# A third sequence's gathers beside the first experts, and an earlier order of fetches in the second attention

## The chip, the cores and the metric

The kernel runs on one core of one Trainium2 chip. The measure is device time in microseconds (us) of one execution; lower is better. Several executions of each kernel are timed, and one more is recorded by the hardware profiler. The engines are called as in the profile: PE is TensorE (matrix multiply; PEld are its weight loads), DVE is VectorE, ACT is ScalarE, POOL is GpSimd, SP is SyncE, which here only issues DMAs. Each engine works through its own instructions in order, and they wait for each other on semaphores. DMAs are issued by SP (plain copies) and by POOL (indirect ones, with an address for each row), and run on 16 DMA engines.

## What is computed

Eight sequences of 512 tokens with 256 features pass through two layers. Each layer is an attention and then a mixture of experts, both with a layernorm ahead and a residual:

```python
x = x + _L0_attn_ref(_layernorm(x, axis=-1), ...)   # 16 heads, 4 key/value heads, rotary, causal
x = x + _L0_ffn_ref(_layernorm(x, axis=-1), ...)    # 32 experts of width 96, 8 per token, weighted sum
x = x + _L1_attn_ref(_layernorm(x, axis=-1), ...)   # 16 heads, causal, biases
x = x + _L1_ffn_ref(_layernorm(x, axis=-1), ...)    # 16 experts of width 176, 2 per token, and a shared one
```

Attention mixes tokens within one sequence only. The experts treat every token by itself: a router picks 8 of 32 (in the second layer 2 of 16) experts for a token, and its result is the weighted sum of theirs.

## The kernel before

**Four stages.** First attention with the first router; first experts; second attention with the second router and the shared expert; second experts. In the profiled execution they take roughly 0 to 370, 370 to 820, 820 to 1366 and 1366 to 1597 us. The attentions go sequence by sequence. The experts go over tiles of 128 rows: the attention stage has scattered each token's row, once for every expert chosen, into a slab of that expert in memory (`xg`, L456 on POOL), and a table says which expert each tile belongs to.

**The first experts (`experts`, L1205).** Two tiles are one job. A job runs through five stages, each a fixed number of steps behind the one before: load the rows from `xg` (SP, L1244), transpose them (PE, L1258), gate and up products (L1290), transpose (L1309), down product (L1319). The result is copied out of PSUM by ACT (`ys`, L1324) and stored to `yg` in memory (SP, L1327). There are 139 jobs, so 146 steps. The order of PE's instructions is fixed by hand; the other engines' order is made by the framework from the order of the code and the dependencies.

**The gathers (`gathers`, L1394).** A token's eight expert results lie in eight rows of `yg`. They are added to its `x` by indirect DMAs with an add: one for each of the 8 choices and each of the 4 groups of 128 tokens, 32 for a sequence, all issued by POOL at L1399. Each fetches 128 rows of 1 KB. Four gathers later the next one adds to the same rows of `x`, and waits until the earlier one has landed. Before that, SP has to fetch `x` itself as it stood after the first attention (`fetch_x`, L168, from `x_after`).

**What may run beside the experts (`Beside`, L1180).** Side work is given as a generator with a first step, a last step and a number of pieces; `Beside.step` takes as many pieces at each expert step as keep it even. `x_in_ring` (L1565) is such work: it fetches `x` of the first `AHEAD` sequences and then makes their gathers, two for each piece, and each of these waits for the last `ys` copy of its step. It runs from step `n_early // 2 + 8` = 83 to the end, 145. Sequences below `AHEAD` read only the first `n_early` = 150 tiles of `yg` (`most_rows`, L1359), which are stored by then; a sequence that isn't read so early waits for all of `yg`. The weights of the second attention are loaded beside these steps too (from step 69).

**The second attention (`planned`, L816).** An outer loop runs over the sequences b = 0 to 7. Each iteration has 12 stages, one for each entry of `PLAN1`; in each, PE makes one block of scores for the heads, and then letters say what side work goes with it: `p` is a piece of the preparation of sequence b + 1 (its layernorm, which reads the gathered `x`, and its projections), `a` and `o` are pieces of the output, the router and the shared expert of sequences b - 1 and b - 2, `g` is a piece of the chain `ahead`, and `m`, `c`, `t` belong to the scores. At the start of each iteration, `ahead` is made for sequence b + `AHEAD` = b + 2: `ahead1` (L1671) fetches its `x`, loads one part of the second experts' gate and up weights (SP), and makes its 32 gathers. The parts are `NB - AHEAD` = 6.

**Five places for x.** `new_x` (L161) takes its tiles from a ring of five. The second attention's sequences 0 to 4 find their places free; sequence 5 has to wait until sequence 0 is through the router and the shared expert and has been copied to memory (`keep_x`, L1687), sequence 6 for sequence 1, and sequence 7 for sequence 2.

**Scatters of the second router.** The router makes 8 scatters for a sequence (2 choices, 4 groups) and appends them to the list `waiting`; in each of the 12 stages `send` issues up to `SENT[1][n]` = 2 of them on POOL, without further waits in this layer.

The lines that steer this:

```python
SENT = ((3, 3, 2), (2, 2, 2))
AHEAD = 2
beside.add(done, end_done, AHEAD * 16 + 1, x_in_ring())        # L1611
"a": chain(finish, b - 1), "g": chain(ahead, b + AHEAD),       # L830
load_gate_up(gw1, f1, I1, N1R, b - AHEAD, NB - AHEAD)          # L1675
```

Marks that are used below: L787 is the first VectorE instruction of a sequence's output, once for each sequence; L344 on `stats_a` is the first step of the layernorm ahead of the second attention; L507 adds the shared expert's result; L735 masks the scores.

Of the kernel before, what the change touches and what calls it, by code (L numbers as in the profile page):

```python
# [8 lines left out]
F32 = mybir.dt.float32  # L9
# [8 lines left out]
P = 128  # L18
NB, T, D = 8, 512, 256
NT = T // P  # L20
# [13 lines left out]
PLAN1 = "cooggm oggm toggm coaggm aopggm taaoggm cppaoggm ppoggm taaopggm caopm aopam tapopm"  # L34
TAIL1 = "otaaoaaaoaoaoaa"
PB = (3, 2)
SENT = ((3, 3, 2), (2, 2, 2))
SPLIT = (4, 6)
AHEAD = 2
GU0, GU1 = ND * 2 * I0, ND * 2 * I1  # L40
ND1 = 2
NS = -(-IS1 // P)
# [56 lines left out]
def two_blocks_kernel(  # L99
# [18 lines left out]
    xpool = ctx.enter_context(tc.tile_pool(name="x", bufs=1, reuse_waits="tile"))  # L118
# [39 lines left out]
    xs = {}  # L158
    x_after = [drp.tile([NB, P, NT * D], F32, tag=f"x_after{n}", name=f"x_after{n}") for n in range(2)]

    def new_x(b, name):  # L161
        xs[b] = xpool.tile([P, NT, D], F32, tag="x", name=f"x_{name}_{b}", bufs=5)
        return xs[b]

    def keep_x(b, dram):
# [2 lines left out]
    def fetch_x(b, dram, name):  # L168
        return nc.sync.dma_start(out=new_x(b, name).rearrange("p t d -> p (t d)"), in_=dram[b]).ins
# [641 lines left out]
    def send(n, pace):  # L811
        for work, t, i in waiting[:n]:
            work(t, i, pace)
        del waiting[:n]

    def planned(att, before, after, plan, tail, ahead=None):  # L816

        def finish(b):
            yield from att.output(b, xs[b])
            yield from after(b)  # L820

        def chain(make, b):
            return make(b) if make and 0 <= b < NB else iter(())

        drain(before(0))
        old, next_one = iter(()), chain(before, 1)
        for b in range(NB):
            chains = {
                "p": next_one, "q": chain(before, b + 2), "o": old,
                "a": chain(finish, b - 1), "g": chain(ahead, b + AHEAD),  # L830
            }
            for at, works in enumerate(plan.split()):
                c, n = divmod(at, len(BANKS))
                if n == 0:
                    att.head(b, c)
                att.scores(b, c, n, att.probs)
                send(SENT[att.n][n], None if att.n else att.newest)
                for work in works:
                    if work == "c":
                        att.products()  # L840
                    elif work == "t":
                        att.turn()
                    elif work == "m":
                        att.mask(n, att.probs)
                    else:
                        next(chains[work], None)
            for work in "pog":
                drain(chains[work])
            next_one, old = chains["q"], chains["a"]
        att.held = att.made  # L850
        att.products()
        chains = {"o": old, "a": finish(NB - 1)}
        for work in tail:
            if work == "t":
                att.turn()
            else:
                next(chains[work], None)
        for work in "oa":
            drain(chains[work])
        if att.n:  # L860
            send(len(waiting), None)
# [497 lines left out]
    def most_rows(b, again):  # L1359
        lay = lays[0]  # L1360
        return (lay.most_tiles if again else lay.n_early if b < AHEAD else lay.n_tiles) * P

# [31 lines left out]
    def gathers(b, again="", pace=None):  # L1394
        lay = lays[0]
        rows = lay.rows[b]
        for i in range(lay.k):
            for t in range(NT):
                inst = nc.gpsimd.indirect_dma_start(  # L1399
                    out=xs[b][:, t, :], out_offset=None, in_=lay.yg[: most_rows(b, again), :],  # L1400
                    in_offset=bass.IndirectOffsetOnAxis(ap=rows[:, t, i : i + 1], axis=0), compute_op=ALU.add,
                )
                if pace:
                    tc.add_manual_dep(inst.ins, pace().name, SYNC, reason="gathers come evenly beside the tiles")
                if t % 2:
                    yield
# [43 lines left out]
    def load_x(b, tmp, bank, xf=None):  # L1450

        new_x(b, "in")
        xf = xf or read_x(b, tmp)
        for h in range(NT // 2):
            tr = bank(f"xin_{b}_{h}").rearrange("p (t d) -> p t d", t=2)
            for i in range(2):
                for c in range(ND):
                    t = 2 * h + i
                    nc.tensor.transpose(tr[:, i, c * P : (c + 1) * P], xf[:, c, t * P : (t + 1) * P], ident)
            nc.scalar.copy(xs[b][:, 2 * h : 2 * h + 2, :], tr)  # L1460
            yield
# [51 lines left out]
    def drain(part):  # L1513
        for _ in part:
            pass
# [31 lines left out]
    def all_experts(n, gw, gat, again=False, weights=()):  # L1547
# [6 lines left out]
        with ExitStack() as s:  # L1554
# [10 lines left out]
            def x_in_ring():  # L1565
                for b in range(AHEAD):
                    fetch_x(b, x_after[0], f"a1{g}")
                yield
                for b in range(AHEAD):
                    yield from gathers(b, g, None if again else lambda: beside.made)  # L1570

            def all_places():
                for b in range(NB):
                    yield from places(b, gat, g, beside.last)
# [34 lines left out]
            if n == 0:  # L1609
                beside.add(*((end + 1, end + 2) if again else (known, done - 2)), NB, all_places())  # L1610
                beside.add(done, end_done, AHEAD * 16 + 1, x_in_ring())  # L1611
            else:
# [17 lines left out]
    with ExitStack() as s2:  # L1630
        lasting.append(s2.enter_context(tc.tile_pool(name="xn_rows", bufs=2, reuse_waits="tile")))
        PARTS = 4
        with ExitStack() as s:
            awp, lnp, atp, late, ptp, smp, ps = pools(s, 0, False)
            bank = banks(ps, 3)
            att, before = fast0(awp, lnp, atp, late, ptp, ps, bank)
            route, _ = ffn_parts(smp, bank)
            gw0 = gpool.tile([P, E0 * GU0], F32, tag="gu", name="gw0")

            def after0(b):  # L1640
                if b == NB - 1:
                    return
                kept = keep_x(b, x_after[0])
                yield from routed0(b, lnp, bank, route)
                if b < PARTS:
                    with tc.issue_after(kept):
                        load_gate_up(gw0, f0, I0, N0, b, PARTS)
                if b == 1:
                    yield from biases1(smp, bank)
                if b == SPLIT[0] - 1:  # L1650
                    yield from tables(lays[0], smp, bank, 0)


            with tc.manual_schedule(engines={ENG.PE}):
                planned(att, before, after0, PLAN0, TAIL0)


        with ExitStack() as s1:
# [4 lines left out]
            with ExitStack() as s:  # L1663
# [7 lines left out]
                def ahead1(b):  # L1671
                    if b >= AHEAD:
                        fetched = fetch_x(b, x_after[0], "a1")
                        with tc.issue_after(fetched):
                            load_gate_up(gw1, f1, I1, N1R, b - AHEAD, NB - AHEAD)  # L1675
                        yield
                        yield from gathers(b)
# [13 lines left out]
                with tc.manual_schedule(engines={ENG.PE}):  # L1691
                    planned(att, before, after1, PLAN1, TAIL1, ahead1)
# [246 lines left out]
```

## Time and profile before

| | |
|---|---|
| median of 3 runs | 1592.55 us (1592.25 to 1599.87) |
| the profiled execution | 1599.16 us, of which the span on the core is 1597.4 |
| mean granted clock of PE | 0.956 |
| PE busy | 1429.2 us, 89% of the span |
| DVE, ACT, POOL busy | 954.7, 667.1, 805.5 us |
| gathers (L1399), on POOL | 256, together 403.5 us |
| scatters (L456), on POOL | 320, together 322.4 us |
| DMA | 240.36 MB, mean 150 GB/s |

The table of groups gives, for a line, the busy time, the mean of one in ns, and the idle time of its engine just before, with what ended it. The table by stretch gives for each stretch the busy time of each engine and the number of its instructions, then the granted clock of PE (1.00 is full), the share of time in which the 16 DMA engines were busy with packets (it can pass 1, as packets overlap), and what they moved. In a timeline each row is a start, a duration, the instruction, and in brackets how long the engine had been idle before it and what ended the wait. The table of DMA queues has packets, MB and the share of 16 engines; `hardware_dynamic` are the copies that SP issues, `software_dynamic` the indirect ones of POOL.

### The profile page before, as it was taken

The page shows a single profiled execution, that of the slowest core. Times are in us where ns is not written, and L with a number is a line of the kernel's source. Part 1 is how long each engine was busy: PE and PEld are TensorE (multiplying, and loading weights), DVE is VectorE, ACT ScalarE, POOL GpSimd, SP SyncE. Part 2 cuts the span into 40 slices and gives each one's busy share as a digit, 9 for nine tenths or more (in the row PEclk, how much of TensorE's full clock was granted, in tenths as well). Part 3 has the DMA queues.
Part 4 walks back from the last instruction along what each step waited for, and adds up shares of the span by engine and source line. Part 5 has one row for each costly group of instructions (what it writes and reads, how often), then busy time and mean ns, then how long its engine had stood idle before and what let it go on. Part 6 is the DMA issues. An engine that isn't in the chain of part 4 may idle for free.

```text
span 1597.4 us, 29845 instructions
## 1 busy us (share of the span) xinstructions
PE 1429.2 (89%) x9856; PEld 971.8 (61%) x9856; DVE 954.7 (60%) x3121; ACT 667.1 (42%) x885; POOL 805.5 (50%) x674
## 2 busy tenths in 40 slices
PE   5899999887888999999997899999798988999994
PEld 3455555545777889999863445545444454677773
DVE  5578888774555566555555657657465664544453
ACT  3566666562232223333324464664544642122221
POOL 0004777774545100365568888888888203233332
PEclk9899999998999999999998999999998988999996
DMA  2024554348778876899995556556454106353365
GB/s 78 14 67 133 170 167 165 120 140 233 254 230 258 264 231 201 216 253 243 256 234 83 70 71 122 112 86 135 80 87 102 45 15 186 102 170 114 113 211 188
DMA packets 230176, 240.36 MB, mean 150 GB/s; under 512 B 77916, under 2 KB 209377, under 8 KB 230018
## 3 DMA queue, kind: packets, MB, share of 16 engines
q1 hardware_dynamic: 173794, 148.87, 31.6%
q0 software_dynamic: 55872, 89.18, 24.6%
q8 instruction: 84, 1.38, 0.4%
q14 instruction: 74, 0.61, 0.1%
q10 hardware_dynamic: 352, 0.33, 0.1%
HBM read 127.36 MB, written 112.49 MB: 150 GB/s over the span
## 4 chain that ended last, share of the span: by engine, by line
PE 49%; POOL 20%; issue 12%; DVE 9%; ACT 5%; DMA 4%; SPq 1%; POOLq 0%; DVEq 0%; ACTq 0%
POOL x_a L1399 16%; PE gu_m L1290 15%; PE y_m L1319 10%; PE st_a L724 5%; PE xgT_m L1258 5%; PE o_a L747 4%; ACT p_a L729 4%; PE hT_m L1309 3%; POOL xg L456 2%; DMA xg<-xn_f,rows_f 2%; DVE p_a L735 2%; POOL yg L1332 1%; PE y_a L802 1%; PE sy_f L502 1%; DMA xg_m<-xg 1%
## 5 line engine op out<-in xcount | busy, mean ns | idle before, releaser
L1399 POOL DMA_INDIRECT x_a<-yg,yrows x256 | 403.5, 1576 | 255.8 <-DMA xg_m<-xg 125.5
L456 POOL DMA_INDIRECT xg<-xn_f,rows_f x320 | 322.4, 1007 | 374.3 <-ACT p_a L729 135.5
L729 ACT ACTIVATE p_a<-st_a 128x2048 f32<-128x2048 f32 (+1 forms) x192 | 306.1, 1594 | 260.2 <-PE st_a L724 151.0
L1290 PE MATMUL gu_m<-gw,xgTs_m 128*128 x1416 | 305.8, 360 | 0.0
L1290 PEld LDWEIGHTS gu_m<-gw,xgTs_m 128*128 128x128 f32 x1416 | 237.3, 194 | 24.7 <-DVE xgTs_m L1260 0.2
L724 PE MATMUL st_a<-qT_a,kT_a 32*128 32x512 f32 (+3 forms) x2048 | 202.6, 489 | 38.2 <-ACT p_a L729 31.1
L1319 PE MATMUL y_m<-dw,hTs_m 96*128 (+1 forms) x860 | 217.8, 383 | 2.3 <-issue 2.3
L735 DVE TENSOR_TENSOR p_a<-p_a,causal 128x512 f32<-128x512 f32 x256 | 170.4, 684 | 80.9 <-ACT p_a L729 80.7
L1260 DVE COPY xgTs_m<-xgT_m 128x512 f32<-128x512 f32 x177 | 121.8, 688 | 100.4 <-PE xgT_m L1258 100.2
L1324 ACT COPY ys_m<-y_m 128x512 f32<-128x512 f32 x177 | 103.6, 585 | 173.6 <-PE y_m L1319 158.4
L747 PE MATMUL o_a<-p_a,v 128*32 128x512 f32 (+3 forms) x2048 | 160.4, 452 | 10.8 <-DVE p_a L735 10.8
L724 PEld LDWEIGHTS st_a<-qT_a,kT_a 32*128 32x128 f32 x2048 | 89.1, 190 | 132.6 <-ACT p_a L729 58.4
L1319 PEld LDWEIGHTS y_m<-dw,hTs_m 96*128 96x128 f32 (+1 forms) x860 | 151.0, 192 | 16.7 <-issue 2.6
L1282 DVE SCALAR_TENSOR_TENSOR h_m<-h_m,xg_m,gu_m 128x96 f32<-128x96 f32 (+1 forms) x354 | 103.9, 325 | 82.0 <-ACT h_m L1295 38.5
L1332 POOL DMA_INDIRECT yg<-ys_m,to_m x76 | 76.4, 1006 | 140.4 <-ACT ys_m L1324 128.0
L747 PEld LDWEIGHTS o_a<-p_a,v 128*32 128x32 f32 x2048 | 57.9, 112 | 135.5 <-issue 98.7
L1258 PE MATMUL xgT_m<-ident,xg_m 128*128 128x128 f32 x708 | 110.5, 279 | 29.7 <-issue 16.7
L1310 DVE COPY hTs_m<-hT_m 96x256 f32<-96x256 f32 (+1 forms) x177 | 84.0, 475 | 81.4 <-PE hT_m L1309 81.4
L1298 ACT ACTIVATE h_m<-gu_m 128x192 f32<-128x192 f32 x139 | 45.9, 330 | 200.5 <-PE gu_m L1290 183.4
L1258 PEld LDWEIGHTS xgT_m<-ident,xg_m 128*128 128x128 f32 x708 | 87.4, 143 | 54.4 <-issue 31.9
L1309 PE MATMUL hT_m<-ident,h_m 128*96 128x128 f32 (+1 forms) x430 | 77.1, 275 | 0.1
L802 PE MATMUL y_a<-wo,oT_a 128*128 128x256 f32 x256 | 65.2, 401 | 11.0 <-DVE x_a L507 10.7
(242 smaller groups left out, 1635.7 us busy)
## 6 DMA issues: line engine op xcount, KB each, us to landing
xg_m<-xg SPq DMA_DIRECT2D x354, 144.0 KB
yg<-ys_m SPq DMA_DIRECT2D x139, 256.0 KB
g<-yg SPq DMA_DIRECT2D x16, 512.0 KB
xg<-zeros SPq DMA_DIRECT2D x50, 144.0 KB
xg<-xn_f,rows_f POOLq DMA_INDIRECT x320
x_after<-x_in SPq DMA_DIRECT2D x8, 512.0 KB
x_a<-x_after SPq DMA_DIRECT2D x8, 512.0 KB
x_a<-yg,yrows POOLq DMA_INDIRECT x256
```

The lines of the kernel that those rows point to most:

```text
L456: inst = nc.gpsimd.indirect_dma_start(out=lay.xg, out_offset=bass.IndirectOffsetOnAxis(ap=rows[:, t, i : i + 1], axis=0), in_=xn[:, t, :], ...
L724: nc.tensor.matmul(st[:, g, at : at + T - j * P], kT[r, j * P : (j + 1) * P], qT[r, j * P :], start=True, stop=True,)
L729: self.newest = nc.scalar.activation(pt, st[:, :, :width], AF.Exp, scale=SCALE).ins
L735: self.masked = nc.vector.tensor_tensor(d, d, causal.unsqueeze(1).to_broadcast([P, NG, P]), ALU.mult).ins
L747: nc.tensor.matmul(o[32 * g : 32 * g + 32, j * P :], v1[:, j, v_at + g * (DH + 1) :][:, :32], probs[n][:, g, at : at + T - j * P], start=( ...
L1258: nc.tensor.transpose(tr[:, j, c, :], xg[:, j, c * P : (c + 1) * P], ident)
L1260: nc.vector.tensor_copy(xT, tr)
L1282: nc.vector.scalar_tensor_tensor(h[:, j, :], h[:, j, :], xg[:, j, D:][:, bass.ds(offs[part, i + j][2], 1)], gus[j][:, inner:], ALU.mult, A ...
L1290: nc.tensor.matmul(gus[j], xT[:, j, c, :], gu[:, bass.ds(at + c * 2 * inner, 2 * inner)], start=(c == 0), stop=(c == ND - 1),)
L1309: nc.tensor.transpose(hp[:n_in, q, j, :], h[:, j, lo : lo + n_in], ident)
L1319: nc.tensor.matmul(y[:, j, :], hT[:n_in, q, j, :], dn[:n_in, bass.ds(at + q * D, D)], start=(q == 0), stop=(q == n_ch - 1),)
L1399: inst = nc.gpsimd.indirect_dma_start(out=xs[b][:, t, :], out_offset=None, in_=lay.yg[: most_rows(b, again), :], in_offset=bass.IndirectOf ...
```

## The change

```diff
-SENT = ((3, 3, 2), (2, 2, 2))
+SENT = ((3, 3, 2), (1, 1, 1))
 SPLIT = (4, 6)
-AHEAD = 2
+AHEAD = 3
+RING = 5
...
     def new_x(b, name):
-        xs[b] = xpool.tile([P, NT, D], F32, tag="x", name=f"x_{name}_{b}", bufs=5)
+        xs[b] = xpool.tile([P, NT, D], F32, tag="x", name=f"x_{name}_{b}", bufs=RING)
         return xs[b]
...
             chains = {
                 "p": next_one, "q": chain(before, b + 2), "o": old,
-                "a": chain(finish, b - 1), "g": chain(ahead, b + AHEAD),
+                "a": chain(finish, b - 1), "g": chain(ahead, b + AHEAD - (b + AHEAD > RING)) if b + AHEAD != RING else iter(()),
             }
```

`AHEAD` is used in five places, and with 3 in place of 2:

- `x_in_ring` fetches `x` of sequences 0, 1 and 2 beside the first experts and makes the gathers of all three there: 96 in place of 64, in 49 pieces in place of 33, over the same steps 83 to 145.
- `most_rows` lets sequence 2 too read the first 150 tiles of `yg` alone.
- In the second attention, iteration 0 fetches and gathers sequence 3 and iteration 1 sequence 4 (2 and 3 before), iteration 2 none (4 before), and iterations 3, 4 and 5 sequences 5, 6 and 7, as before.
- `ahead1` loads the second experts' gate and up weights in five parts in place of six, with sequences 3 to 7 in place of 2 to 7.
- The general path, which recomputes everything if a check at the end fails and isn't run here, has the same edits.

The ring of `x` keeps its five places; `RING` names their number. `SENT` lets each stage of the second attention issue one scatter of the router in place of two, so a sequence's eight scatters spread over eight stages in place of four. The order of PE's instructions and all arithmetic stay as they are.

## The prediction

> **What bounds the kernel now.** I began with the chain of waits, to see which engine other than TensorE stands on the path to the end:
>
> ```profile
> PE 49%; POOL 20%; issue 12%; DVE 9%; ACT 5%; DMA 4%; SPq 1%; POOLq 0%; DVEq 0%; ACTq 0%
> ...
> L1399 POOL DMA_INDIRECT x_a<-yg,yrows x256 | 403.5, 1576 | 255.8 <-DMA xg_m<-xg 125.5
> ```
>
> GpSimd is busy for half of the span only, yet a fifth of the chain lies on it, nearly all in one line: the gathers of the first layer's results (L1399). The busy table by stretch, 20 us a row, says where:
>
> ```profile
> core 0: us, PE busy (x) PEld busy (x) DVE busy (x) ACT busy (x) POOL busy (x), PEclk, DMA share, GB/s
> 600.00:620.00 20.00, 20.00 (x129) 18.64 (x128) 14.39 (x49) 6.41 (x14) 0.00 (x0) 1.00 0.68 196
> 700.00:720.00 20.00, 20.00 (x129) 18.64 (x128) 11.14 (x30) 6.41 (x14) 10.93 (x8) 1.00 1.04 256
> ...
> 980.00:1000.00 20.00, 19.85 (x170) 8.96 (x167) 12.08 (x44) 10.57 (x11) 16.64 (x12) 1.00 0.60 92
> 1000.00:1020.00 20.00, 19.63 (x112) 9.41 (x114) 9.43 (x26) 14.53 (x14) 16.04 (x14) 1.00 0.45 97
> ...
> 1140.00:1160.00 20.00, 9.29 (x53) 6.72 (x45) 8.70 (x29) 3.68 (x4) 16.04 (x14) 0.81 0.45 90
> 1160.00:1180.00 20.00, 19.97 (x132) 11.32 (x136) 14.50 (x42) 6.86 (x7) 16.78 (x11) 0.85 0.55 101
> 1200.00:1220.00 20.00, 16.26 (x104) 8.60 (x103) 7.15 (x15) 13.63 (x12) 16.64 (x12) 0.93 0.51 69
> 1220.00:1240.00 20.00, 16.96 (x106) 10.58 (x106) 16.16 (x55) 4.53 (x5) 15.35 (x16) 0.81 0.44 142
> ```
>
> In the second attention (about 820 to 1366 us) GpSimd never rests up to 1240: 16 us of 20 plus 0.30 us of issue per instruction. TensorE is full all the same until 1140 and then falls short twice. Beside the experts (660 to 820) GpSimd works at half rate, TensorE is full, and the DMA engines are at 1.0, after 0.68 before the gathers began. The timeline of VectorE shows what the two gaps wait for (L787 marks the same place in every sequence, L344 is the first layernorm step, which reads the gathered x):
>
> ```profile
> 1130.62 0.22 DVE L787 SCALAR_TENSOR_TENSOR fine<-rec_a,fine 128x64 f32<-128x64 f32 x1
> 1147.24 0.43 DVE L344 BATCH_NORM_STATS2 stats_a<-x_a 128x6 f32<-128x256 f32 x1 [9.42 <-DMA x_a<-yg,yrows]
> ...
> 1204.64 0.22 DVE L787 SCALAR_TENSOR_TENSOR fine<-rec_a,fine 128x64 f32<-128x64 f32 x1
> 1217.66 0.43 DVE L344 BATCH_NORM_STATS2 stats_a<-x_a 128x6 f32<-128x256 f32 x1 [5.83 <-DMA x_a<-yg,yrows]
> ```
>
> These are sequences 6 and 7: their gathers came too late. The L787 marks stand at 894.06, 951.68, 1010.76, 1070.07, 1130.62, 1204.64 and 1273.61; the distances are 57.6, 59.1, 59.3, 60.6, 74.0 and 69.0 us.
>
> One coincidence has to be seen through. In the timeline of GpSimd the gathers stand 1.847 us apart (1.54 of work, 0.30 of issue), so 32 take 59.1 us, just what an undisturbed iteration takes. But in those iterations TensorE is busy 19.6 to 19.9 us of 20 and VectorE doesn't wait for x. TensorE sets the 59.1; GpSimd needs 59.1 for the gathers and another 10.7 for eight scatters (1008.43 to 1019.09), and so falls behind until sequences 6 and 7 must wait.
>
> **What the Trainium skill says.** "DMA: Bandwidth & Descriptors", section "Issuing engines are not separate DMA queues", says that all issuers share the same 16 DMA engines and interleave. This trace agrees: from 740 to 820 us the two queues together fill them.
>
> ```profile
> q1 hardware_dynamic: 21559, 15.96, 67.3%
> q0 software_dynamic: 4237, 3.85, 33.6%
> ```
>
> "Perfetto Trace Analysis", section "DMA Instruction — SWDGE (GPSIMD)", says that the recorded end of such an instruction is the end of making descriptors, not of moving data. Agreed: a gather shows 1.54 us at a DMA share of 1.04 and at 0.5 alike, so GpSimd's row won't show crowding. "TensorE: Matmul & The Clock Gate", section "HAM oscillation — how this bites in real kernels", says that idle gaps above about 3.4 us bring the slow clock back. Here, after gaps of 6.97 and 3.74 us, the granted clock is 0.81 and 0.85, so a gap costs more than its length.
>
> **The change, part by part.**
>
> *No change to TensorE's order.* It is fixed by hand, and no edit touches a call that issues to it.
>
> *1. Gathers removed from the attention.* In the run before, sequence 2's gathers are issued from 825.97 to 887.6 us, ahead of sequences 3 to 7; these 32 x 1.847 = 59.1 us leave GpSimd's queue. To undo both waits GpSimd has to be earlier by their sum. I take 59.1 us as the undisturbed iteration: 74.0 - 59.1 = 14.9, 69.0 - 59.1 = 9.9, 60.6 - 59.1 = 1.5, together 26.3 us. The clock is within this, since it comes from whole iterations. VectorE's wait of 2.42 us at 902.80 for gathered rows goes as well; part of TensorE's idle there is waiting for exponentials, so 0 to 2, taken as 1. Gain: 27 us.
>
> *2. Is anything late next?* The 96 gathers beside the experts need 96 x 1.847 = 177.3 us from 655.1, so they end at 832 at the earliest, 8 later than the 64 did. Sequence 3 then takes GpSimd to 891, sequence 4 to 950. Sequence 5 needs sequence 0's place: its copy to memory was issued at 968.72 and the fetch at 972.50, so gathers can begin at about 975 and end at 1034. Sequence 6's place comes at 1033.6 (the fetch of that time), so with ten us of scatters it runs to about 1104, sequence 7 from 1114 to 1173. Layernorm wants them at 1077, 1137.8 and 1137.8 + 59.1 = 1196.9. All are early, sequence 7 by 23 us. That is also the tolerance: sequence 3 could start some 25 us later before a wait returns. The pause without gathers costs nothing; TensorE covers it.
>
> *3. Gathers added beside the experts.* 30 gathers took 33.6% of 80 us of all engines, 0.90 us each; 32 are 28.7 us of DMA, and the third fetch (512 KB at some 250 GB/s) 2. Over the 168 us from 655 to 823 this raises the share from 1.00 to about 1.18. What the engines can do isn't shown directly. Below: the stretch 755 to 760 reached 1.20, so 1.18 may fit, cost 0. Above: if 1.00 is the limit, the stage grows by 31 us. The nearest evidence is in the pace: the copies at L1324 come every 2.826 us, and 62 steps from 640 to 815 slipped by only 2.7 us in sum though the share was 1.0, so the experts' prefetch isn't used up. The best row over 20 us is 1.07. If 1.12 lasts, (1.18 / 1.12 - 1) x 168 = 9 us of excess, and gathers left over at the end may slip past it within the tolerance of step 2. I take 6.
>
> *4. GpSimd's pace there.* 49 steps of the generator over 62 expert steps are a pair every 1.265 x 2.826 = 3.58 us against 3.69 needed: GpSimd is just full, and lags by a few us, which is in the 832. A gather waits for TensorE's stage, not the reverse; only later gathers and sequence 3 queue behind it.
>
> *5. SENT (1, 1, 1).* The same eight scatters of 1.27 us for each sequence, spread over eight stages; sequences 0 to 5 are wanted only by the second experts after 1366. Cost 0; if they displaced a gather it would be by 10 us, inside the 23.
>
> *6. Weights in five parts instead of six.* The same bytes on SP's queue, each part a fifth bigger, the last still with sequence 7's fetch. In the attention the DMA share is 0.5, so 0.
>
> Sum: -27 + 6 = -21 us. The profiled execution took 1599.16 (span 1597.4, 1.8 around it), which would become 1578; it stands 6.6 above the median of the runs, 1592.55, from which I forecast 1571.6, say 1572.
>
> **Rivals.**
> - *Crowded DMA eats part of it* (0.17). The stage grows by 10 to 25 us, net 2 to 17 gained: 1576 to 1590, middle 1583. For: share 1.04 already. Against: only 2.7 us of slip.
> - *The gathers don't fit and spill* (0.12). They add to the same rows, so each waits for the one four before it. If landings slow down, GpSimd ends sequence 2 at about 887 as before, and nothing moves: 1592. For: two waits of GpSimd for x_a's own DMA at 715 and 721. Against: they are 4.5 us in sum, and no longer than their neighbours'.
> - *The experts become DMA-bound and cold* (0.14, the slower side). If about 1.00 is a hard limit, the stage grows by 31 us, and TensorE's gaps lower the clock as at 440 to 450 us (0.70): 31 / 0.85 = 36, plus some 3 more at the crossing to attention; 1592.5 - 27 + 39 = 1604. It decides once the growth exceeds 27.
> - *The forecast* (0.57): 1561 to 1581.
>
> **Numbers.** About 0.5% (8 us) is what can be told from no change: below 1584.6 is faster. Faster: 0.57 + 0.11 of the first rival + 0.03 of the second = 0.71; same: 0.06 + 0.08 = 0.14; slower 0.15. The range 1561 to 1597 leaves out the third rival and the tails; the likeliest case alone has 1561 to 1581.
>
> **What would show it.** Right: L787 marks 58 to 60 us apart throughout, no wait of L344 for x_a over 2 us, x_a's gathers at two thirds of GpSimd's time beside the experts, and a pause on GpSimd around 950 to 975. Wrong: L1324 copies over 3.0 us apart after 655 (crowding), sequence 2's last gather after 865 (spill), or iterations still of 70 us.

## The result, and the profile after

The changed kernel takes 1575.30 us (median of 6 runs, 1563.25 to 1584.12) against 1600.71 us of the kernel before in the same comparison (6 runs, 1592.25 to 1605.98). The ratio is 0.985, with a 95% interval of 0.980 to 0.990. The three further runs of the kernel before lie higher than the three that the prediction started from (1592.55), so the 25.4 us of gain end near the forecast time of 1572 although the forecast gain was 21. The profiled execution went from 1599.16 to 1577.96 us, its span from 1597.4 to 1576.2: 21.2 us less, the mean granted clock of TensorE 0.963 in place of 0.956. The lines of the code stand one higher than before: the gathers are L1400, the layernorm step is L345, the mark of each sequence L788, the `ys` copies L1325.

The page of the changed kernel, the chain of waits and, of the costliest groups, the line of the gathers:

```profile
PE 60%; DVE 12%; issue 8%; POOL 7%; ACT 7%; DMA 4%; SPq 1%; DVEq 0%; ACTq 0%; POOLq 0%
...
L1400 POOL DMA_INDIRECT x_a<-yg,yrows x256 | 405.3, 1583 | 214.1 <-DMA wq<-in_a_dram 122.8
```

The same 256 gathers cost GpSimd the same 1.58 us each, and GpSimd is busy as long as before (812.1 us in place of 805.5). But its share of the chain has fallen from 20% to 7%, and TensorE's has risen from 49% to 60%. Nothing became cheaper; work left the path.

The timeline of VectorE in the changed kernel, at the two places where it waited before:

```profile
1077.87 0.21 DVE L788 SCALAR_TENSOR_TENSOR fine<-rec_a,fine 128x64 f32<-128x64 f32 x1
1137.07 0.22 DVE L788 SCALAR_TENSOR_TENSOR fine<-rec_a,fine 128x64 f32<-128x64 f32 x1
1144.19 0.42 DVE L345 BATCH_NORM_STATS2 stats_a<-x_a 128x6 f32<-128x256 f32 x1
...
1196.34 0.21 DVE L788 SCALAR_TENSOR_TENSOR fine<-rec_a,fine 128x64 f32<-128x64 f32 x1
1203.46 0.42 DVE L345 BATCH_NORM_STATS2 stats_a<-x_a 128x6 f32<-128x256 f32 x1
1255.31 0.21 DVE L788 SCALAR_TENSOR_TENSOR fine<-rec_a,fine 128x64 f32<-128x64 f32 x1
```

The layernorm steps of sequences 6 and 7 carry no bracket any more, so they waited for nothing. This row of the waits view of before (us in total, times, longest) has no counterpart after:

```profile
DVE stats_a L344 <- DMA x_a<-yg,yrows: 25.7, 10, 9.4
```

From the second to the sixth distance the marks stand 59 us apart:

| distance of the marks, us | 1 | 2 | 3 | 4 | 5 | 6 | 7 | sum |
|---|---|---|---|---|---|---|---|---|
| before | 57.62 | 59.08 | 59.31 | 60.55 | 74.01 | 68.97 | 45.43 | 424.97 |
| after | 56.55 | 59.01 | 59.17 | 59.20 | 59.27 | 58.97 | 43.96 | 396.12 |

So the second attention is 28.85 us shorter between its first and last mark. The first mark comes 9.08 us later (894.06 to 903.14), and the stretch from the last mark to the end is 1.4 us shorter (278.4 to 277.0). The sum is -28.85 + 9.08 - 1.4 = -21.2 us.

Where the 9.08 arose has to be measured from a point that is the same work in both kernels. The first gather is not: 96 gathers over the same steps begin one step earlier than 64, 0.86 us after the 79th `ys` copy in place of 0.86 us after the 80th, and a step is 2.83 us. Counted from the 79th copy:

| us | before | after | difference |
|---|---|---|---|
| start to the 79th `ys` copy | 651.41 | 657.65 | 6.24 |
| from there to the first layernorm of the second attention | 166.95 | 170.03 | 3.08 |
| from there to the first mark | 75.70 | 75.46 | -0.24 |

The 6.24 were already there at the 49th copy (566.64 and 572.88), before anything that the change touches, so they belong to the difference between two executions. The 3.08 are what the stretch with the gathers took more in this pair. The table by stretch shows what happens beside the experts after the change:

```profile
core 0: us, PE busy (x) PEld busy (x) DVE busy (x) ACT busy (x) POOL busy (x), PEclk, DMA share, GB/s
700.00:720.00 20.00, 19.20 (x123) 17.64 (x122) 10.38 (x28) 6.16 (x14) 16.72 (x11) 1.00 1.11 258
720.00:740.00 20.00, 20.00 (x129) 18.58 (x128) 11.16 (x29) 6.42 (x14) 16.64 (x12) 1.00 1.14 280
740.00:760.00 20.00, 18.85 (x120) 16.97 (x118) 10.21 (x27) 6.37 (x14) 16.64 (x12) 1.00 1.10 250
```

GpSimd is now full there (11 or 12 gathers in 20 us, 7 or 8 before), the DMA share is 1.10 to 1.14, and TensorE is short of full by about 1 us in two of the three rows, with the clock at 1.00. The DMA queues from 740 to 820 us of the changed kernel:

```profile
q1 hardware_dynamic: 21181, 15.51, 63.6%
q0 software_dynamic: 5933, 5.41, 45.5%
```

The gathers' queue has 40% more packets than before (5933 to 4237), that of SP slightly fewer (21181 to 21559), and the two queues together come to 109% in place of 101%.

GpSimd's timeline where sequence 5 has to wait for its place in the ring:

```profile
961.94 1.54 POOL L1400 DMA_INDIRECT x_a<-yg,yrows  x1 [0.30 <-issue]
963.79 1.04 POOL L457 DMA_INDIRECT xg<-xn_f,rows_f  x1 [0.30 <-issue]
...
973.11 0.99 POOL L457 DMA_INDIRECT xg<-xn_f,rows_f  x1 [0.31 <-issue]
983.88 1.58 POOL L1400 DMA_INDIRECT x_a<-yg,yrows  x1 [9.78 <-DVE w_f L317]
```

The last gather ahead of sequence 5 is issued at 961.94, eight scatters follow in one block, and then GpSimd stands still for 9.78 us, until SP has fetched sequence 5's x (issued at 979.75). The releaser that the row names, a VectorE instruction, is the one that the profile saw last; that the fetch is what was waited for is inferred from its place just ahead. The gathers of sequences 6 and 7 (at 1055.39 and 1126.52) start 0.3 us after the scatter ahead of them, so they don't wait for their places: from 983.88 on GpSimd's own pace sets the start of gathers again.

### The profile page after: what moved, and what is told of

Same layout as the page of the kernel before. It is cut to its first block, busy times and chain, and to the rows that moved or that the text cites. A ratio compares the mean times of both kernels' runs of the same rounds, so it can differ in the third digit from the quotient of the medians.

```text
span 1576.2 us, 29855 instructions
## 1 busy us (share of the span) xinstructions
PE 1423.1 (90%) x9856; PEld 971.5 (62%) x9856; DVE 950.8 (60%) x3121; ACT 667.3 (42%) x885; POOL 812.1 (52%) x674
## 3 DMA queue, kind: packets, MB, share of 16 engines
q0 software_dynamic: 55872, 89.18, 24.5%
## 4 chain that ended last, share of the span: by engine, by line
PE 60%; DVE 12%; issue 8%; POOL 7%; ACT 7%; DMA 4%; SPq 1%; DVEq 0%; ACTq 0%; POOLq 0%
PE gu_m L1291 15%; PE y_m L1320 10%; PE st_a L725 7%; PE o_a L748 6%; POOL x_a L1400 5%; PE xgT_m L1259 5%; ACT p_a L730 4%; PE hT_m L1310 3%; DVE p_a L736 2%; PE sy_f L503 2%; PE sg_f L490 2%; PE su_f L490 2%; PE k_a L1057 1%; POOL xg L457 1%; PE y_a L803 1%
## 5 line engine op out<-in xcount | busy, mean ns | idle before, releaser
L457 POOL DMA_INDIRECT xg<-xn_f,rows_f x320 | 327.0, 1022 | 389.1 <-ACT p_a L730 134.2
L1400 POOL DMA_INDIRECT x_a<-yg,yrows x256 | 405.3, 1583 | 214.1 <-DMA wq<-in_a_dram 122.8
L1325 ACT COPY ys_m<-y_m 128x512 f32<-128x512 f32 x177 | 103.7, 586 | 178.1 <-PE y_m L1320 160.1
```

Source lines behind the costliest of these rows:

```text
L457: inst = nc.gpsimd.indirect_dma_start(out=lay.xg, out_offset=bass.IndirectOffsetOnAxis(ap=rows[:, t, i : i + 1], axis=0), in_=xn[:, t, :], ...
L1400: inst = nc.gpsimd.indirect_dma_start(out=xs[b][:, t, :], out_offset=None, in_=lay.yg[: most_rows(b, again), :], in_offset=bass.IndirectOf ...
```

## The experiments

Each edit is shown against the changed kernel. Kernels of one comparison ran on the same chip with the kernel before beside them.

**One part alone.** `SENT` goes back to (2, 2, 2), and each of the sequences 3 and 4 is asked for one iteration later, as before. Only the third sequence's gathers beside the experts and the weights in five parts remain.

```diff
-SENT = ((3, 3, 2), (1, 1, 1))
+SENT = ((3, 3, 2), (2, 2, 2))
...
-"g": chain(ahead, b + AHEAD - (b + AHEAD > RING)) if b + AHEAD != RING else iter(()),
+"g": chain(ahead, b + 2 if b else NB),
```

> AHEAD = 3 is kept, SENT goes back to (2, 2, 2), and sequences 3 and 4 are asked for in iterations 1 and 2, as before the change. Theory (only the 32 gathers beside the experts count, since GpSimd takes its queue as fast as it can whatever iteration an instruction was written in): as the changed kernel, near 1575 us, L788 marks 59 us apart, no wait of the layernorm for x. Rival (the earlier order of 3 and 4, or the slower scatters, carry part of the gain): gathers of sequence 3 start some 40 us later than 840, waits of 10 us or more come back before sequences 6 and 7, 1585 to 1600 us.

Measured: 1572.23 us against 1597.93, ratio 0.9852 (0.9816 to 0.9888): the ratio of the whole change. The marks sum to 397.1 us (after: 396.1), and the layernorm waits for no gather. The order of instructions explains why the parts add nothing: setting only `SENT` back gives the same sequence of instructions on every engine as the changed kernel, and so does asking for sequences 3 and 4 an iteration later, while `SENT` (1, 1, 1) put alone into the kernel before gives that kernel's sequence. The framework orders the queues of GpSimd and SP by itself: the gathers of sequences 3 and 4 are mixed with each other there (in the trace between 840 and 962 us), and the scatters of a sequence stay one block of eight. `AHEAD` is the whole change, and this run is the changed kernel's program a second time.

**The third sequence's gathers left out.**

```diff
 for b in range(AHEAD):
-    yield from gathers(b, g, None if again else lambda: beside.made)
+    if b < 2 or again:
+        yield from gathers(b, g, None if again else lambda: beside.made)
...
-beside.add(done, end_done, AHEAD * 16 + 1, x_in_ring())
+beside.add(done, end_done, 2 * 16 + 1, x_in_ring())
```

> The changed kernel without sequence 2's 32 gathers: its x lacks the first experts' results; 64 gathers in 33 pieces run beside the experts, as before the change, and the attention starts with sequence 3. Theory (the DMA crowding from the added gathers costs some 6 us): from the first gather to sequence 0's layernorm 163 to 164 us in place of 169.2, DMA share there 1.0 in place of 1.1, marks unchanged at 59 us, some 6 us below the changed kernel: 1568 to 1570. Rival (the longer stage is chance or comes from elsewhere): 168 us or more, and the time of the changed kernel.

Measured: 1570.86 us, 0.9837 (0.9806 to 0.9868): 1.4 us below the first experiment, whose interval overlaps, and not the 6 us expected. From the first gather to the first layernorm 164.6 us, with a DMA share of 0.997. The attention is as in the changed kernel (marks sum to 398.5). Counted from the 79th `ys` copy, as above, the stretch takes 168.3 us here, 167.0 in the first experiment and 170.0 in the changed kernel. So these three don't show that the 32 gathers beside the experts cost anything; all profiles together are taken up in point 3 below.

**Half of the third there, half at the head of the attention's queue.**

```diff
-    def gathers(b, again="", pace=None):
+    def gathers(b, again="", pace=None, some=slice(None)):
...
-        for i in range(lay.k):
+        for i in range(lay.k)[some]:
...
-                    yield from gathers(b, g, None if again else lambda: beside.made)
+                    half = slice(0, 4) if b == 2 and not again else slice(None)
+                    yield from gathers(b, g, None if again else lambda: beside.made, half)
...
-                beside.add(done, end_done, AHEAD * 16 + 1, x_in_ring())
+                beside.add(done, end_done, 40 + 1, x_in_ring())
...
                     if b >= AHEAD:
+                        if b == AHEAD:
+                            yield from gathers(2, some=slice(4, 8))
```

> Only the first 16 of sequence 2's gathers beside the experts, the other 16 at the head of the attention's. Theory: half of the crowding (2 to 4 us less than the changed kernel), and GpSimd, some 15 us later than there, still early enough for sequence 7: no wait over 2 us, 1571 to 1574 us. Rival (the lead is already used up): waits for x of sequences 6 and 7 come back, 10 us or more together, 1580 or more.

Measured: 1567.86 us, 0.9815 (0.9785 to 0.9845); the interval overlaps that of the first experiment. From the first gather to the first layernorm 163.5 us (167.2 from the 79th copy), no waits for x. A second comparison is told below.

**The attention's weights loaded earlier.** They come in expert steps 55 to 83, so that they don't share the DMA engines with the gathers.

```diff
-                lay.n_tiles // 4, end, len(weights), weights_loaded(),
+                *((lay.n_tiles // 5, done) if weights else (lay.n_tiles // 4, end)), len(weights), weights_loaded(),
```

> The changed kernel with the second attention's weights loaded in expert steps 55 to 83 in place of 69 to 145, that is ahead of the gathers. Theory (what costs is the sum of all DMA work while the gathers run): the share while they run falls from 1.11 to about 1.06, first gather to layernorm 164 to 167 us in place of 169.2, 2 to 4 us less in all unless the steps 55 to 83 slow down by as much. Rival (the gathers alone hold the copies up, whatever else is on the queue): 169 us as in the changed kernel.

Measured: 1571.26 us, 0.9832 (0.9800 to 0.9864). The share from the first gather on fell from 1.108 in the first experiment to 1.067 (that from 575 to 655 us rose from 0.727 to 0.841), but the stretch from the 79th copy to the first layernorm took 166.5 us, only 0.5 less than the 167.0 of the first experiment. The 30 steps ahead of it took 84.9 us against 84.8, so the earlier loads cost nothing to speak of. The 0.5 us is less than the 3 us between two executions of the changed program (167.0 and 170.0), so no gain from a lower sum of DMA work shows here, and that the sum is what costs isn't shown.

**More gathers for sequence 3: 16, then 32.** The first 4, or all 8, of its choices are gathered twice, so that GpSimd gets 29.5 or 59.1 us more to do at the head of the attention's queue.

```diff
-        for i in range(lay.k):
+        for i in [*range(4 if b == AHEAD and not again else 0), *range(lay.k)]:
```

> The changed kernel with the first 16 of sequence 3's gathers made twice (its x gets half of the first experts' results a second time), which puts GpSimd back by 16 x 1.85 = 29.5 us from 840 on. Theory (GpSimd's lead over the layernorms is all that matters in the attention, and the changed kernel has some 30 us of it to spare, counting the pause before sequence 5): sequence 7's last gather at about 1198 with its layernorm wanted at 1203; waits of the layernorms for x of 0 to 3 us, 0 to 4 us above the changed kernel: 1572 to 1579. Rival (each gather in the attention costs time of its own, by DMA or memory contention with TensorE's feeding): 29 us at 1 to 1, or at least 10: 1583 or more.

> The same with all 32 of sequence 3's gathers made twice (its x gets the first experts' results twice), 59 us for GpSimd, which takes back just the lead that the change gave. Theory: the waits of before come back in sum, 20 to 30 us, at the first layernorm that GpSimd is late for (sequence 3's, since its own gathers are doubled), 1593 to 1605 us. Rival (gathers cost time of their own): 59 us, 1630; or none (something else of the change made the gain): 1575.

Measured with 16: 1579.39 us against 1600.35, 0.9864 (0.9812 to 0.9916). The timeline of VectorE:

```profile
1189.30 0.21 DVE L788 SCALAR_TENSOR_TENSOR fine<-rec_a,fine 128x64 f32<-128x64 f32 x1
1196.71 0.43 DVE L345 BATCH_NORM_STATS2 stats_a<-x_a 128x6 f32<-128x256 f32 x1 [0.21 <-DMA x_a<-yg,yrows]
1200.43 0.43 DVE L345 BATCH_NORM_STATS2 stats_a<-x_a 128x6 f32<-128x256 f32 x1 [1.38 <-DMA x_a<-yg,yrows]
1202.28 0.43 DVE L345 BATCH_NORM_STATS2 stats_a<-x_a 128x6 f32<-128x256 f32 x1 [1.35 <-DMA x_a<-yg,yrows]
1252.67 0.22 DVE L788 SCALAR_TENSOR_TENSOR fine<-rec_a,fine 128x64 f32<-128x64 f32 x1
```

Only sequence 7 is late, and only just: waits of 2.9 us in sum, and 63.4 us between the two marks in place of 59.0. Of the added 29.5 us, 13.5 arrived at the last gather (1184.9 to 1198.4). Of the rest, 9.5 went into the pause ahead of sequence 5, which is 0.30 us here, and in this execution the 96 gathers beside the experts ended 5.0 us earlier.

Measured with 32: 1609.06 us, 1.0056 (1.0036 to 1.0076): slower than before, and above the 1593 to 1605 expected. The waits view and the timeline, then the table by stretch:

```profile
DVE stats_a L345 <- DMA x_a<-yg,yrows: 31.9, 8, 21.1
```

```profile
983.91 0.43 DVE L345 BATCH_NORM_STATS2 stats_a<-x_a 128x6 f32<-128x256 f32 x1 [21.11 <-DMA x_a<-yg,yrows]
```

```profile
core 0: us, PE busy (x) PEld busy (x) DVE busy (x) ACT busy (x) POOL busy (x), PEclk, DMA share, GB/s
940.00:960.00 20.00, 19.63 (x123) 7.68 (x125) 11.21 (x45) 15.04 (x13) 16.64 (x12) 1.00 0.51 71
960.00:980.00 20.00, 6.33 (x64) 4.40 (x56) 1.30 (x2) 4.82 (x4) 16.69 (x11) 0.72 0.52 73
980.00:1000.00 20.00, 11.27 (x44) 8.36 (x44) 12.12 (x37) 1.02 (x1) 16.90 (x11) 0.68 0.56 93
```

The added work comes back as one long wait of sequence 3's own layernorm, 21.11 us (24.5 with the three short ones behind it), and its iteration grows from 59.0 to 84.2 us, by 25.2. The other 7.4 us of waits come at sequence 7. The granted clock falls to 0.72 and 0.68, which agrees with what the section "HAM oscillation — how this bites in real kernels" of the Trainium skill's page "TensorE: Matmul & The Clock Gate" says, that idle gaps above about 3.4 us bring the slow clock back (TensorE's longest gap here is 18.65 us). Beyond the waits themselves the iteration grows by little, 0.7 us. The marks sum to 428.2 us, close to the 425.0 of before. With the lead gone, nothing of the gain is left.

**No gathers in the second attention.** The `yield from gathers(b)` of `ahead1` is removed, so sequences 3 to 7 enter without the first experts' result, and GpSimd has only the scatters left.

> The changed kernel without any gather of sequences 3 to 7: their x lacks the first experts' results. Theory (TensorE sets the 59 us of an iteration, and that 32 gathers take 59.1 us too is chance): L788 marks still 58 to 60 us apart, the time within 5 us of the changed kernel's, 1569 to 1577. Rival (GpSimd's 59 us set the iteration): marks 50 to 56 us apart, 1555 or less.

Measured: 1571.16 us, 0.9806 (0.9753 to 0.9859). The marks stand 54.6, 58.8, 59.0, 59.0, 59.0, 59.0 and 44.0 us apart. The table by stretch:

```profile
core 0: us, PE busy (x) PEld busy (x) DVE busy (x) ACT busy (x) POOL busy (x), PEclk, DMA share, GB/s
980.00:1000.00 20.00, 19.93 (x161) 8.72 (x159) 12.02 (x48) 11.15 (x12) 0.00 (x0) 1.00 0.00 1
1000.00:1020.00 20.00, 19.63 (x126) 9.84 (x125) 9.27 (x26) 14.06 (x13) 7.71 (x8) 1.00 0.17 60
1020.00:1040.00 20.00, 19.22 (x141) 13.11 (x141) 18.75 (x60) 9.51 (x10) 0.00 (x0) 1.00 0.41 119
```

GpSimd has nothing but its scatters, the DMA engines are at most at 0.41, and an iteration takes 59 us all the same, with TensorE at 19.2 to 19.9 of 20. The 160 gathers that the changed kernel still has there cost 2.7 us in the sum of the marks (396.1 to 393.3), of which 2.0 lie in the first distance.

**The change and the half version once more.** The unedited changed kernel and the half version, compared directly.

> The changed kernel itself once more, beside the next run on the same chip, to set the size of chance: theory 1570 to 1577 us, marks 59 us apart, and 163 to 170 us from the first gather to sequence 0's layernorm (two executions with the same instructions gave 169.2 and 166.1).

> Half of sequence 2's gathers beside the experts, once more and on the same chip as the changed kernel. Theory (half of the crowding is saved, no wait comes back): 2 to 5 us below the changed kernel of this call. Rival (the difference of the first runs was chance): within 1 us of it, either way.

This comparison ran on another chip, and there the kernels take 7% longer: the kernel before 1707.56 us, the changed one 1700.48, ratio 0.9946 (0.9928 to 0.9963), the half version 1705.30, 0.9977 (0.9955 to 0.9998). So the half version isn't shown to be better than the change: its median is 4.8 us above it, where 2 to 5 below or no difference was expected. It was 2.9 us shorter beside the experts (166.8 us from the 79th `ys` copy to the first layernorm, 169.7 with the change), and lost more in the attention (its marks sum to 433.2 us, those of the change to 425.6).

The gain shrinks on this chip from 1.5% to 0.5%. The marks of the changed kernel stand 56.9, 61.9, 63.3, 70.5, 69.2, 59.8 and 44.0 us apart, although no layernorm waits for x. The first attention is longer too, from the first scatters on. Two rows of this trace, one of ScalarE's timeline and one of VectorE's, and the rows of TensorE around them:

```profile
1225.27 1.88 ACT L730 ACTIVATE p_a<-st_a 128x2048 f32<-128x2048 f32 x1 [5.02 <-remote]
```

```profile
1225.25 0.23 DVE L393 TENSOR_REDUCE top_f<-lg_f 128x4 f32<-128x64 f32 x1 [4.16 <-remote]
```

```profile
1215.81 1.15 PE L725 MATMUL st_a<-qT_a,kT_a 32*128 32x384 f32 x16
1218.34 0.33 PE L390 MATMUL lg_f<-ident,turn_f 128*128 128x128 f32 x1 [1.38 <-ACT turn_f L387]
1218.50 1.88 PE L1052 MATMUL q_a<-xT_a,wq 128*128 128x512 f32 x4
1227.19 1.24 PE L725 MATMUL st_a<-qT_a,kT_a 32*128 32x256 f32 x8 [6.81 <-ACT p_a L730]
```

By TensorE's rows the operands were ready (`st_a` ended at 1216.96, `lg_f` at 1218.67), but the ends of these rows are modelled, not observed. "remote" says only that the view found no releaser. The semaphore events kept with the trace tell more: both engines waited for the semaphore that TensorE's instructions raise, and only they. By the events kept it rose at 1219.44 and then not until 1225.19 and 1225.23, 4.8 us after the last end of TensorE's rows, and both engines went on within 0.05 us. So the two engines stop together here because both wait for TensorE, whose signal comes late. The same holds for all 69 rows with this releaser in the four traces of the slower chips: each wait ends within 0.1 us of a rise of that semaphore, 1.5 to 6.3 us after the last recorded end of an instruction that raises it. (Those traces lack about a sixth of these events, 286 of 1666 in this one, against 9 at most on the faster chips, so their releasers are to be read with care.)

Rows with this releaser don't occur in the traces of the faster chips. Here the second attention has 7 of them, 23.5 us in sum, and the first attention 13; the experts have none, though GpSimd issues gathers beside them too. The long iterations are those in which GpSimd issues gathers, though not all such iterations are long: the first has gathers throughout and takes 56.9 us. Two more kernels were recorded for this: the kernel before, and the one without gathers in the attention.

> The kernel before, recorded once more, because the last call's chip was 7% slower and no profile of the kernel before was taken there. There the iterations of the second attention in which GpSimd issues indirect DMAs took 62 to 71 us with the change. Theory (where iterations are stretched to GpSimd's own pace, there is little lag to remove): on such a chip the kernel before has iterations of some 66 to 72 us from the first on, GpSimd's 59.1 us of gathers and some 10.7 us of scatters fit into them, and VectorE waits for gathered x under 10 us in sum instead of 25.7; the time is near 1707. Rival (the stretching comes with the change): iterations of 59 us up to sequence 5, then waits of 9.4 and 5.8 us as before. On a chip of the faster kind this run only repeats the profile of before: near 1597, with the waits at sequences 6 and 7.

> The changed kernel without the gathers of sequences 3 to 7, recorded once more: their x enters the second attention as the first attention left it. Theory (on the slower chip GpSimd's indirect DMAs stretch the work of VectorE and ScalarE): there the second attention runs at 59 us per iteration once GpSimd has nothing to issue but eight scatters, and the time is 40 to 60 us under that of the changed kernel there (1700), near 1650. Rival (the slow chip is slower for everything): iterations of 62 us and more with GpSimd idle, near 1695. On a chip of the faster kind this run only repeats the earlier one: near 1571.

Both ran on a fourth chip, again of the slower kind: the kernel before took 1705.0 us beside them. One execution of each was recorded, so their totals are rough. Without the attention's gathers the time is 1674.04 us, and the marks stand 54.7, 59.5, 59.7, 59.7, 59.7, 59.8 and 45.4 us apart, 398.6 in sum. Its table by stretch:

```profile
core 0: us, PE busy (x) PEld busy (x) DVE busy (x) ACT busy (x) POOL busy (x), PEclk, DMA share, GB/s
1200.00:1220.00 20.00, 19.93 (x162) 9.05 (x154) 11.38 (x48) 11.42 (x11) 2.88 (x3) 1.00 0.04 16
1220.00:1240.00 20.00, 18.93 (x127) 10.67 (x126) 11.47 (x37) 14.95 (x14) 5.00 (x5) 1.00 0.13 46
```

So on this kind of chip, too, TensorE needs 59.7 us for an iteration, and no engine shows a stop of that sort in the second attention any more (its first attention still has 18 such rows). With the gathers the changed kernel's marks sum to 27 us more, 425.6 - 398.6, though on another chip of this kind (the expected 40 to 60 was too much). On the faster chips the same removal changed the sum by 3 us.

The kernel before (1697.64 us) has 57.3, 59.9, 62.0, 63.7, 66.5, 79.1 and 42.7 us between its marks, 431.2 in sum, and its layernorm waits for x for 15.6 us. The longest of these waits:

```profile
1306.23 0.43 DVE L344 BATCH_NORM_STATS2 stats_a<-x_a 128x6 f32<-128x256 f32 x1 [5.04 <-DMA x_a<-yg,yrows]
```

That lies between what the theory (under 10) and the rival (25.7) asked for. Iterations grow already without the change, by less than the theory said; while they are longer, GpSimd lags less, and less of the old wait is left to remove (5.6 us at sequence 6, 8.4 at sequence 7). The change removes both, but its own fourth and fifth iterations are 70.5 and 69.2 us. The difference of the sums is 431.2 - 425.6 = 5.6 us on two chips of this kind, in place of 28.9. Why TensorE's signals come late on some chips, what the gathers have to do with it, and why the changed kernel has more of it in two iterations, stays open. As each chip was used once, and the two slower ones last, the hour isn't ruled out as the cause either.

## Why the prediction was right, point by point

**1. The lead of GpSimd (27 us).** Right, in place and nearly in size: 28.85. The two long iterations gave 14.7 and 10.0 us (predicted 14.9 and 9.9), the fourth 1.35 (1.5), the other four 2.75 together (1). The three doses put beside each other show that it is the lead that counts, and not something else in the change: 0, 16 and 32 more gathers ahead of sequence 3 give waits for x of 0, 2.9 and 31.9 us. That TensorE and not GpSimd sets the 59 us, which the prediction read from busy columns, is shown by the kernel without gathers. One reading was off without harm: sequence 2's gathers were not ahead of the others in GpSimd's queue from 825.97 to 887.6. By the order of instructions they were mixed with those of sequence 3, four to one, and the last ended at 901.1, which fits the wait of sequence 2's own layernorm at 902.80. The 59.1 us that leave the queue are the same. That a gap costs more than its length holds, but only just: the two long iterations of before lost 24.7 us for 22.3 us of waits, the one with 32 more gathers 25.2 for 24.5.

**2. What is late next: nothing.** Right, with a smaller margin. Sequence 5's fetch was foreseen at 972.5 and came at 979.75, since the whole attention started 9 us later; its first gather came at 983.88 (975). Sequence 7's gathers were to end at 1173 and ended at 1186.4; the layernorm came at 1203.5 in place of 1196.9. So the slack was 17 us and not 23: the gathers of sequences 5, 6 and 7 begin 71 us apart (983.9, 1055.4, 1126.5), for 59.1 of gathers and some 10.7 of scatters, while the layernorms come every 59, and the prediction had them 70 apart from an earlier start. The tolerance to a delay ahead of sequence 3, put at some 25 us, is just under 29.5: the pause ahead of sequence 5 takes up the rest.

**3. The crowding (6 us).** Too large, and this is the term that luck covered. From the 79th `ys` copy to the first layernorm, all profiles, weights early left aside:

| gathers beside the experts | us |
|---|---|
| 64 | 167.0, 167.0, 168.3 |
| 80 | 166.8, 167.2 |
| 96 | 167.0, 167.6, 168.5, 168.9, 169.7, 170.0, 172.4 |

The means are 167.2 for the first two rows together and 169.2 for the third: about 2 us, with ranges that overlap. The same program alone gave 167.0, 169.7 and 170.0. That the DMA engines are what costs these 2 us is argued, not shown: with the weights early the share fell by 0.04 and the stretch by 0.5 us only. The prediction took 1.12 as what the DMA engines can sustain, with nothing but a 5 us stretch to go by, and priced what lies above. They held 1.09 from the first gather to 815 us (1.01 before), at up to 1.14 in 20 us, and moved 261 GB/s in place of 248 there. The rivals in which 1.0 is a hard limit (the experts cold, 1604; the third sequence's gathers ending at 887) fall: the clock beside the experts is 1.00 and its gathers ended at about 840.

**4. GpSimd's pace.** Right: 16.6 of 20 us busy plus 0.30 us of issue for each gather. The end came at 840, for 832, of which 3.4 us were there from the first gather on.

**5. SENT, and 6. the weights in five parts.** Right at 0, for a stronger reason than the one given in step 5. The eight scatters aren't spread over eight stages at all; the sequence of instructions is the same with (2, 2, 2). That the iteration in which sequences 3 and 4 are asked for doesn't matter either is shown by the same comparison. The weights in five parts were never tried apart; nothing in the trace waits for them.

**The sum.** -27 + 6 = -21 foreseen, -21.2 measured in the profiled pair. That the two agree so closely is luck. The attention gave 1.9 us more than foreseen and the end of the kernel 1.4, and the stretch with the gathers cost 3.1 in place of 6; without the 6.2 us by which this execution was late before the gathers began, the pair would stand at -27.4. The medians, at -25.4 here and -25.7 for the same program in the first experiment, are nearer to that. The mechanism was right, the crowding was overpriced. The prediction doesn't say that the gain depends on the chip: on the two slower ones the attention gained 5.6 us, since iterations with gathers take up to 70.5 us there, and TensorE's work alone 59.7.

## What to carry to other kernels

When a queue of side work falls behind a little in each iteration, the loss shows only in the last iterations, and the cure is a head start as long as the sum of the waits, taken where that engine is idle. Measure the head start by adding work of a known length until the wait returns. When two engines show the same cadence, take the work of one away to see which sets it; here removing 160 gathers took 3 us on one kind of chip and 27 us on the other. Measure a stretch from an instruction that the change doesn't move: counted from the first gather, which came a step earlier, the cost beside the experts looked like 5 us and is about 2. Where a view names no releaser for a wait, ask which semaphore ended it. A gain measured on one chip needn't be that of another.

## What the runs showed of the hardware that was not expected

- The packets of the DMA queues summed to 1.09 of the 16 engines for 150 us, and to 1.14 in 20 us, while the experts lost about 2 us; a share of 1.0 is not the limit.
- The same kernel took about 1600 us on two chips and about 1706 us on two others, with iterations of the second attention equal to within about 1% (59.0 and 59.7 us) once GpSimd has no gathers to issue. On the slower ones ScalarE and VectorE, at times both at once, wait some microseconds for a signal of TensorE that comes 1.5 to 6.3 us after the recorded end of its work. This is seen in both attentions, and no longer in the second once its gathers are gone, though its scatters stay. Beside the experts it isn't seen.
